# Column sums of k taken in column tiles directly behind the products they belong to, relu of the next k moved beside them, a sixth convolution bank, and GpSimd in a written order

## The chip, the cores and the metric

The kernel runs on one core of one Trainium2 chip. The metric is the device time of one launch in microseconds, the median of three runs. Everything is float32.

## The reference, cut to what matters

Two layers are applied to x of shape (8, 256, 64, 64). The first is an attention over keys and values that come from a strided 4x4 convolution; it is not touched here. The second is a linear attention with a multi-scale branch:

```python
qkv = einsum('oc,bchw->bohw', w_qkv, x)                     # 3 * 256 channels
dw  = depthwise 5x5 convolution of qkv, padding 2
agg = einsum('goi,bgihw->bgohw', w_pw, dw grouped by 8)     # 96 groups of 8
ms  = concatenate([qkv, agg], axis=1)
# per head of 8 channels: q, k, v of ms over the 4096 positions n
q, k = relu(q), relu(k);  v = [v, 1]                        # a column of ones
kv  = einsum('bhnd,bhne->bhde', k, v)                       # 8 x 9
out = einsum('bhnd,bhde->bhne', q, kv)
out = out[..., :-1] / (out[..., -1:] + 1e-15)
p   = einsum('oc,bchw->bohw', w_proj, att), scaled and shifted; result x + p
```

The ninth column of kv is the sum of relu(k) over all positions, since v is padded with ones. These column sums of k, once for the k of qkv ("raw") and once for that of the branch ("agg"), are what the change moves.

## The kernel before

The kernel has three passes. The first does layer one and stores q, k and v of the second layer in forms that the second can load. The second pass computes the convolved q and k and the sums kv. The third divides and projects.

The second pass works on 64 units, `(t, k, b)`: two halves of the channels, four groups of 32 channels in each, eight images. The function `second_pass` is a loop over `u`, in which unit `u` is convolved (k of the branch), unit `p = u - 1` has its sums taken, and pairs of units have their q convolved in "products" (`m`, one pair in two iterations). Thus an even iteration has four products and an odd one has five. One iteration on TensorE is:

- `convolve(u, 2)` (L1372), then `products(u, 0)` (L1403)
- `convolve(u, 0)`, then `products(u, 1)`
- `summed_raw(u)` (L1441): 32 matmuls of relu(k) against v in 32-wide column tiles, into the bank `raw`
- `summed(p)` (L1458): 32 matmuls with 288 columns in column tiles, into the bank `sums`
- `ended_raw(u)` (L1482): the column sum of raw k, one full-array matmul with `ones` as the weights' partner, into a column of `raw`
- `convolve(u, 1)`
- `ended(p)` (L1494): the column sum of the branch's k, one full-array matmul into the bank `few`
- `products(u, 2)`

Convolutions and products write to five banks tagged `cv`, in turn. With one bank each for `raw`, `sums` and `few` that is all eight.

GpSimd does, for each unit, three additions that fold k to one 128x128 block before its column sum (`reduced`: `red_raw` and `red_agg`, L1352 to L1354), the copy `c` of `paired(u, 2)` (L1299), and half of each `y` of `down` (L1325): `y_1` from the loaded grid `d`, `y_0` and `y_2` from differences `c0` that VectorE made in `across` (L1309). Once for each set of weights it also makes a quarter of the product weights `w` (`widened_q`, L603); VectorE makes another quarter and ScalarE, in 16 small activations (L613), the rest. These 18 steps are "chores" handed out by `do(n)` at fixed places of the iteration; `wide` marks the iterations with a set of product weights, and the other chores are `widened_k` (L592).

ScalarE applies relu to k in place (`positive`, L1359), copies and relus the convolution results (L1381, L1389, L1409). VectorE adds up what comes out of the banks (L1388, L1421, L1428, L1431), and turns `sums` into kv with `taps` (L1468 to L1475). SP issues every load and store: `d` for the k convolution (L1259), `kq` (L1273) and eight `vq` loads (L1285), two halves of `d` for the products (L1267), and the stores of kv (L1490, L1500) and q (L1508).

The order on each engine is made by a scheduler from its own estimate of when operands are ready. `tc.keep_in_program_order(i)` is an exception: it sets `i` behind the one instruction that was written just before it for the same engine. A pin on an instruction whose predecessor is itself free therefore pins it to little.

Of the kernel before, what the change touches and what calls it, by code (L numbers as in the profile page):

```python
# [29 lines left out]
ALU = mybir.AluOpType  # L30
# [568 lines left out]
def widened_q(tc, w, wd, ws):  # L599
    nc = tc.nc  # L600
    n = w.shape[1]
    for g in (2, 3):
        (nc.vector if g == 2 else nc.gpsimd).tensor_tensor(  # L603
            w[:, :, g].rearrange("p n (o f) -> p n o f", o=D1),
            wd[:, g].unsqueeze(2).to_broadcast([P, n, D1, R * R]),
            ws[:, g].unsqueeze(1).unsqueeze(3).to_broadcast([P, n, D1, R * R]),
            ALU.mult,
        )
        yield
    for g in (0, 1):  # L610
        for o in range(D1):
            tc.keep_in_program_order(
                nc.scalar.activation(  # L613
                    w[:, :, g, o * R * R : (o + 1) * R * R], wd[:, g], AF.Copy, scale=ws[:, g, o : o + 1]
                )
            )
            yield
# [595 lines left out]
def second_pass(ctx: ExitStack, tc: tile.TileContext, a, planes, kd, vd, kept, first_w, kvd, kvg, qd, ahead):  # L1213
    nc = tc.nc
    B = a.x.shape[0]
    def pool(name, bufs=1):
# [8 lines left out]
    )  # L1225
    psums = {
        tag: ctx.enter_context(tc.tile_pool(name=f"psum_{tag}", bufs=1, space=bass.MemoryType.PSUM))
        for tag in ("cv", "raw", "sums", "few")
    }

    def bank(tag, name, bufs=1, n=512):
        return psums[tag].tile([P, n], F32, tag=tag, name=name, bufs=bufs)
# [59 lines left out]
    def paired(u, i):  # L1292
        d = grids[u]
        c = cells[u, i] = pairs.tile([P, 4, (NB + 1) * NB // 2], F32, tag=f"c1_{i}", name=f"c1_{u}_{i}")
        v = c.rearrange("p g (y x) -> p g y x", x=NB // 2)
        d0, d1, d2 = (d[:, :, :, i : i + NB - 1 : 2] for i in range(3))
        if i == 2:

            nc.gpsimd.tensor_copy(v, d1)  # L1299
        else:  # L1300
            nc.vector.tensor_sub(v, d2 if i else d0, d1)

# [13 lines left out]
    def down(m, j):  # L1316


        c = column(m, j).rearrange("p g b y x -> p (g b) y x")
        y = quads.tile([P, 2, 4, P], F32, tag="y", name=f"y_{m}_{j}", bufs=2)  # L1320
        setattr(quad[m], f"y{j}", y)
        v = y.rearrange("p i g (b y x) -> p i (g b) y x", b=2, y=NB // 2)
        c0, c1, c2 = (c[:, :, i : i + NB - 1 : 2] for i in range(3))
        nc.vector.tensor_sub(v[:, 0], c0, c1)
        nc.gpsimd.tensor_tensor(v[:, 1], c2, c1, ALU.subtract)  # L1325

    load_cells(0)
    load_tokens(0)
# [15 lines left out]
    ones = const.tile([P, 1], F32, tag="ones", name="ones")  # L1344
    nc.vector.memset(ones, 1.0)

    kts, reds, raws, mraws, state, maggs = {}, {}, {}, {}, {}, {}


    def reduced(u, what, t):  # L1350
        r = mid.tile([P, 4, P], F32, tag=f"red_{what}", name=f"red_{what}_{u}", bufs=1)
        nc.gpsimd.tensor_tensor(r, t[0], t[1], ALU.add)  # L1352
        nc.gpsimd.tensor_tensor(r[:, :2], r[:, :2], r[:, 2:], ALU.add)
        nc.gpsimd.tensor_tensor(r[:, 0], r[:, 0], r[:, 1], ALU.add)  # L1354
        reds[u, what] = r[:, 0]

    def positive(u):
        kq = kqs[u]
        tc.keep_in_program_order(nc.scalar.activation(kq, kq, AF.Relu))  # L1359
        reduced(u, "raw", (kq[:, 0], kq[:, 1]))  # L1360

    def convolve(u, i):
        t, k, b = units[u]
        c, w = cells[u, i], wt[t, k]
        ps = bank("cv", f"cv1_{u}_{i}", 5)
        for g in range(4):
            for da in range(2):
                n = 2 * da + i if i < 2 else 4 + da  # L1370
                cols = slice(da * (NB // 2), da * (NB // 2) + P)
                nc.tensor.matmul(  # L1372
                    ps[:, g * P : (g + 1) * P],
                    c[:, g, cols],
                    w[:, g, n * P : (n + 1) * P],
                    start=(da == 0),
                    stop=(da == 1),
                )
        if i == 2:
            both = between.tile([P, QB], F32, tag="both", name=f"both1_{u}")  # L1380
            nc.scalar.copy(both, ps)  # L1381
            r = (second if u % 2 else sides).tile([P, 2, 4, P], F32, tag="r1", name=f"r1_{u}", bufs=1)
            state[u] = (r, both)
            kts[u] = r
        else:
            r, both = state[u]
            s = sides.tile([P, QB], F32, tag="s", name=f"s1_{u}_{i}")
            nc.vector.tensor_add(s, ps, both)  # L1388
            nc.scalar.activation(r[:, i].rearrange("p h n -> p (h n)"), s, AF.Relu)  # L1389


    def product(m, i, j):
        t, k, b = units[2 * m]
        now, w = quad[m], wq[t, k, (i, j)]
        ps = bank("cv", f"cv0_{m}_{i}{j}", 5)
        for g in range(4):
            out = ps[:, g * P : (g + 1) * P]
            if i == 1:
                x = column(m, j)[:, g, :, 1:NB:2]
                out = out.rearrange("p (b y x) -> p b y x", b=2, y=NB // 2)  # L1400
            else:
                x = getattr(now, f"y{j}")[:, i // 2, g]
            nc.tensor.matmul(out, w[:, g], x, start=True, stop=True)  # L1403

        def piece(name):
            return quads.tile([P, QB], F32, tag=name, name=f"{name}_{m}")

        def finished(v, y, x):
            nc.scalar.activation(  # L1409
                now.r.rearrange("p h b (y i x k) -> p i k (h b) y x", y=NB // 2, i=2, k=2)[:, y, x],  # L1410
                v.rearrange("p (n y x) -> p n y x", y=NB // 2, x=NB // 2),
                AF.Relu,
            )

        if (i, j) == (1, 1):
            now.both = between.tile([P, QB], F32, tag="both", name=f"both0_{m}")
            nc.scalar.copy(now.both, ps)
        elif j == 1:
            v = piece(f"side{i}")
            setattr(now, f"side{i}", v)  # L1420
            nc.vector.tensor_add(v, ps, now.both)  # L1421
        elif i == 1:
            now.r = now.r if j else late.tile([P, 4, 2, NK], F32, tag="r0", name=f"r0_{m}")
            for y in (0, 2):
                side = getattr(now, f"side{y}")
                v = side if j else piece(f"part{y}")
                setattr(now, f"part{y}", v)
                nc.vector.tensor_add(v, ps, side)  # L1428
        else:
            v = getattr(now, f"part{i}")  # L1430
            nc.vector.tensor_add(v, v, ps)  # L1431
            finished(v, i // 2, j // 2)


    def summed_raw(u):
# [11 lines left out]
                )  # L1447
        raws[u] = ps


    def summed(u):
        kt, vq = kts.pop(u), vqs.pop(u)
# [2 lines left out]
        for i in range(8):  # L1455
            par, r, c = i // 4, i // 2 % 2, i % 2
            for h in range(4):
# [4 lines left out]
                    start=(i == 0),  # L1462
                    stop=(i == 7),
                )
        t, k, b = units[u]
        reduced(u, "agg", (kt[:, 0].rearrange("p h n e -> p n h e"), kt[:, 1].rearrange("p h n e -> p n h e")))
        p = small.tile([P, 36, D1], F32, tag="p", name=f"p_{u}", bufs=1)
        nc.vector.tensor_mul(p, ps[:, : 36 * D1].rearrange("p (n e) -> p n e", e=D1), taps[t][:, k])  # L1468
        s = small.tile([P, D1], F32, tag="kv", name=f"kv_{u}")
# [3 lines left out]
        nc.vector.tensor_mul(x, mix[:, 4 * t + k], s.unsqueeze(1).to_broadcast([P, D1, D1]))  # L1473
        m = small.tile([P, D1 + 1], F32, tag="m", name=f"m_{u}")
        nc.vector.tensor_reduce(m[:, :D1], x, AX.X, ALU.add)  # L1475
        maggs[u] = m

    def ended_raw(u):
        t, k, b = units[u]
        ps = raws.pop(u)  # L1480
        col = ps[:, 64:65]
        nc.tensor.matmul(col, reds.pop((u, "raw")), ones, start=True, stop=True)  # L1482
        m = small.tile([P, D0 + 1], F32, tag="mraw", name=f"mraw_{u}")
        nc.vector.tensor_copy(m[:, :D0], ps[:, :D0])
        nc.vector.tensor_copy(m[:, D0:], col)
        mraws[u] = m

    def stored_raw(u):
        t, k, b = units[u]
        tc.keep_in_program_order(nc.sync.dma_start(kvd[b, t][:, k], mraws.pop(u)))  # L1490

    def ended(u):
        col = bank("few", f"few_{u}")[:, :1]
        nc.tensor.matmul(col, reds.pop((u, "agg")), ones, start=True, stop=True)  # L1494
        nc.vector.tensor_copy(maggs[u][:, D1:], col)

    def stored_agg(u):
        t, k, b = units[u]
# [30 lines left out]
        j = t + 2 * what  # L1529
        parts[j, k] = factors(nc, kept if what else w_q, a, j, k, 6 if what else 9)  # L1530

    positive(0)
    load_factors(0, 0)
    for i in (2, 0, 1):
        paired(0, i)
    for u in range(n_all + 3):
        p, q = u - 1, u - 2
        now, was, conv = u < n_all, 0 <= p < n_all, 0 <= q < n_all
# [14 lines left out]
        if conv and u % 2 == 0:  # L1553
            across(q // 2, 0)
            down(q // 2, 1)
        if u < 2:
            chores.append(weights_q(0, u))
        if now:
# [16 lines left out]
        if u == n_all:  # L1575
            next(ahead)
        if u == n_all + 1:
            ahead.send(lambda name: bank("cv", name, 5))
        if conv and u % 2:
            down(q // 2, 2)  # L1580
        products(u, 0)
# [6 lines left out]
            down(q // 2, 0)  # L1588
            across(q // 2, 2)
        products(u, 1)  # L1590
        do(3 if wide else 2)
        if now:
            summed_raw(u)
        if was:
            summed(p)
        if now:
            ended_raw(u)
            do(6 if wide else 2)
            convolve(u, 1)
        if u + 1 < n_all:  # L1600
            paired(u + 1, 1)
# [3 lines left out]
            load_tokens(2)  # L1605
        if was and p == n_all // 2 - 1:
            load_taps(1)
        if was:
            ended(p)
        products(u, 2)  # L1610

        if u + 1 < n_all:
            positive(u + 1)
        do(9 if wide else 0)
    ahead.send(lambda name: bank("cv", name, 5))

# [472 lines left out]
```

## Time and profile before

| | |
|---|---|
| median of 3 runs | 3550.98 us (3549.43 to 3553.87) |
| profiled execution | 3553.7 us, span 3551.9 us |
| TensorE matmuls busy | 3473.5 us, 98% of the span |
| VectorE, ScalarE, GpSimd busy | 2286.0 (64%), 1478.6 (42%), 1854.5 (52%) |
| mean granted TensorE clock | 0.990 |
| DMA | 647.28 MB, mean 182 GB/s; about 260 GB/s in the second pass |
| second pass | first convolution at 1931.50 us, last sums near 2902 us |

In the lines of the profile, `PE` is TensorE's matmul, `PEld` its weight load, `DVE` VectorE, `ACT` ScalarE, `POOL` GpSimd and `SPq` SyncE's DMA queue. A line of the timeline has start, duration of the merged group, engine, source line, operation, output and inputs, shape and count, and in brackets the idle time ahead of it with what ended it. Matmul ends are modelled, so lengths on TensorE are best read from start to start. One float32 matmul shows as two records. A line of waits has the waiter, what it waited for, microseconds in total, times and the longest.

### The profile page before, as it was taken

What the parts mean: (1) busy time and instruction counts of PE and PEld (TensorE: products, weight loads), DVE (VectorE), ACT (ScalarE), POOL (GpSimd) and SP (SyncE); (2) the same over time, 40 slices, a digit from 0 to 9 for tenths busy, and PEclk for the clock granted to TensorE, in tenths of its full rate; (3) what the DMA queues carried; (4) which work ended last, traced back from release to release, by engine and by line L of the source; (5) the groups of instructions that cost most, each with busy time, mean ns of one, the idle gap of its engine ahead of it and who ended that gap; (6) DMA issues with size and microseconds to landing.
All of it is one profiled execution on the core that took longest, in us unless ns stands there. A gap on an engine that the chain in (4) does not pass through costs nothing.

```text
span 3551.9 us, 91328 instructions
## 1 busy us (share of the span) xinstructions
PE 3473.5 (98%) x38050; PEld 2110.9 (59%) x38050; DVE 2286.0 (64%) x3507; ACT 1478.6 (42%) x3385; POOL 1854.5 (52%) x1754
## 2 busy tenths in 40 slices
PE   7999999999999999999998999999999999999998
PEld 5554655555545555555445888888888873343333
DVE  1567576576675765756777777777777784444443
ACT  2445344353453543535553444444444322333332
POOL 2556466465564664655664566565656542222221
PEclk9999999999999999999999999999999998999999
DMA  5445446355354463553656999999999988788773
GB/s 174 111 104 163 116 114 173 99 159 148 100 161 117 115 172 99 159 148 103 161 126 157 266 262 259 263 258 260 262 263 256 261 233 229 215 242 235 227 225 95
DMA packets 577192, 647.28 MB, mean 182 GB/s; under 512 B 81664, under 2 KB 452864, under 8 KB 576768
## 3 DMA queue, kind: packets, MB, share of 16 engines
q1 hardware_dynamic: 576768, 641.34, 64.9%
q8 instruction: 301, 4.93, 0.6%
q14 instruction: 123, 1.01, 0.1%
HBM read 389.85 MB, written 249.23 MB: 180 GB/s over the span
## 4 chain that ended last, share of the span: by engine, by line
PE 86%; DMA 5%; DVE 3%; SPq 2%; ACT 2%; issue 1%; POOL 1%; DVEq 0%; ACTq 0%; POOLq 0%
PE qkv L994 16%; PE p L1806 12%; PE sc L847 8%; PE cv L1372 7%; PE av L879 7%; PE sr L750 6%; PE o L947 6%; PE q L829 6%; PE cv L1403 6%; PE sums L1458 6%; DMA vq<-v 2%; PE av L905 2%; PE rep L1790 2%; DMA d<-planes 1%; PE den L1771 1%; PE raw L1441 1%
## 5 line engine op out<-in xcount | busy, mean ns | idle before, releaser
L860 ACT ACTIVATE e<-sc 128x512 f32<-128x512 f32 x1024 | 528.6, 603 | 508.3 <-PE sc L847 508.3
L899 POOL TENSOR_TENSOR ef<-ef,e 128x512 f32<-128x512 f32 x512 | 688.3, 1354 | 91.1 <-ACT e L860 67.8
L892 POOL TENSOR_TENSOR ef<-e 128x512 f32<-128x512 f32 x256 | 329.6, 1307 | 544.2 <-ACT e L860 544.1
L1372 PE MATMUL cv<-w,c 128*128 128x128 f32 x3072 | 385.2, 278 | 6.7 <-DVE stage L1007 4.0
L1816 POOL TENSOR_TENSOR y<-z,xs 128x512 f32<-128x512 f32 x120 | 156.9, 1307 | 427.0 <-ACT z L1814 413.1
L1372 PEld LDWEIGHTS cv<-w,c 128*128 128x128 f32 x3072 | 362.6, 193 | 8.5 <-issue 4.1
L847 PE MATMUL sc<-q,kk 32*64 32x256 f32 x8192 | 298.5, 387 | 5.6 <-ACT e L860 5.2
L994 PE MATMUL qkv<-differences,combined 128*128 128x512 f32 x576 | 288.7, 592 | 0.6 <-POOL differences L964 0.6
L926 DVE STREAM_TRANSPOSE rden<-av 128x256 f32<-128x256 f32 x256 | 99.7, 428 | 283.8 <-ACT att L917 236.3
L1458 PE MATMUL sums<-vq,r 128*32 128x288 f32 x4096 | 266.1, 408 | 0.8 <-issue 0.8
L1389 ACT ACTIVATE r<-s 128x512 f32<-128x512 f32 x128 | 80.9, 632 | 422.3 <-DVE s L1388 419.9
L1814 ACT ACTIVATE z<-p,bn 128x512 f32<-128x512 f32 x128 | 99.5, 777 | 372.9 <-PE p L1806 372.9
L879 PE MATMUL av<-e,vv 64*32 64x256 f32 x8192 | 252.4, 379 | 0.1
L847 PEld LDWEIGHTS sc<-q,kk 32*64 32x64 f32 x8192 | 155.3, 131 | 163.0 <-issue 101.4
L1806 PE MATMUL p<-raw,wp 128*128 128x512 f32 x512 | 247.5, 605 | 2.2 <-ACT wp L1742 2.2
L750 PE MATMUL sr<-x,wsr 128*128 128x256 f32 x1024 | 237.2, 385 | 11.6 <-DMA wsr<-in_w_sr_dram 11.6
L829 PE MATMUL q<-x,wq 128*128 128x512 f32 x512 | 241.9, 594 | 0.0
L1806 PE MATMUL p<-agg,wp 128*128 128x512 f32 x512 | 240.4, 592 | 0.0
L750 PEld LDWEIGHTS sr<-x,wsr 128*128 128x128 f32 x1024 | 196.3, 193 | 67.5 <-issue 40.9
L947 PE MATMUL o<-att,wout 128*128 128x512 f32 x512 | 230.3, 592 | 0.0
L932 DVE TENSOR_TENSOR att<-att,rall 128x512 f32<-128x512 f32 x128 | 217.6, 1700 | 4.4
L1010 DVE TENSOR_TENSOR whole<-part,qkv 128x512 f32<-128x512 f32 x256 | 172.3, 683 | 66.1 <-ACT part L1060 49.4
(164 smaller groups left out, 6073.9 us busy)
## 6 DMA issues: line engine op xcount, KB each, us to landing
planes<-stage SPq DMA_DIRECT2D x128, 578.0 KB
d<-planes SPq DMA_DIRECT2D x128, 578.0 KB
vq<-v SPq DMA_DIRECT2D x256, 256.0 KB
raw<-planes SPq DMA_DIRECT2D x64, 578.0 KB
x<-in_xp_dram SPq DMA_DIRECT2D x64, 512.0 KB
wsr<-in_w_sr_dram SPq DMA_DIRECT2D x128, 256.0 KB
x<-x SPq DMA_DIRECT2D x128, 256.0 KB
k<-turned SPq DMA_DIRECT2D x256, 128.0 KB
```

The lines of the kernel that those rows point to most:

```text
L750: nc.tensor.matmul(ps[:, oc], w[:, ci, oc * P : (oc + 1) * P], strips(b, f // 2)[:, ci, f % 2 * NK : (f % 2 + 1) * NK], start=(f == ci == ...
L829: nc.tensor.matmul(ps, consts["wq"][:, ci, c * P : (c + 1) * P], strips(b, s)[:, ci], start=(ci == 0), stop=(ci == 1),)
L847: nc.tensor.matmul(scs[h][HALVES[half], QH[kq % 2]], kks[b][rows, c, kq * P // 2 : (kq + 1) * P // 2], qs[rows, QH[half]], start=True, sto ...
L860: nc.scalar.activation(e[:, h % 2].rearrange("p q n -> p (q n)"), scs[h], AF.Exp, scale=D0**-0.5)
L879: nc.tensor.matmul(sums["av"][half][cols, : QB // 2], vvs[b][rows, kq, c * P + h * D0 : c * P + (h + 1) * D0], es[h // 2][rows, h % 2, kq ...
L892: tc.keep_in_program_order(nc.gpsimd.tensor_tensor(f, e[:, :, 0], e[:, :, 1], ALU.add))
L899: tc.keep_in_program_order(nc.gpsimd.tensor_tensor(f, f, e[:, :, half], ALU.add))
L947: nc.tensor.matmul(ps, consts["wout"][:, c, oc * P : (oc + 1) * P], att[c], start=(c == 0), stop=(c == 1))
L994: nc.tensor.matmul(ps, w, x, start=True, stop=True)
L1372: nc.tensor.matmul(ps[:, g * P : (g + 1) * P], c[:, g, cols], w[:, g, n * P : (n + 1) * P], start=(da == 0), stop=(da == 1),)
L1458: nc.tensor.matmul(ps[h * D0 : (h + 1) * D0, : 36 * D1].rearrange("p (r n e) -> p r n e", r=3, e=D1), kt[:, par, h, 2 * r + c], vq[:, r : ...
L1806: nc.tensor.matmul(as_block(ps, i // 2), wp[:, i, oc * P : (oc + 1) * P], block(g, i // 2, i % 2, j), start=(i == 0), stop=(i == 3),)
```

## The change

Six things are done, all in `second_pass`.

- The two column sums become `counted`: four matmuls each, one per 32-column tile, with one column of output, written to a free column of the bank of the products they belong to (`raw`, column 32; `sums`, column 288). Both stand right behind `summed(p)`. The bank `few` is gone, and the kv tail reads the column from the `sums` bank; raw kv is copied in one piece of 33 columns.
- The bank that came free goes to the convolutions: six `cv` banks.
- `reduced_agg(p)` is written near the start of the iteration, where before the additions were written behind `summed(p)`.
- `positive(u + 1)` and `reduced_raw(u + 1)` move from the end of the iteration to just behind the column sums, ahead of `convolve(u, 1)`. For unit 0 they are written behind `load_factors` and `paired`.
- The chores of an iteration stand 3, 3, 13 (wide) or 2, 2, 4, all ahead of the sums, where they were 3, 3, 3, 6, 9 or 2, 2, 2, 2.
- Every GpSimd instruction of the pass is pinned with `keep_in_program_order`: `c`, `y`, the `red` additions and `w`.

```diff
@@ widened_q
-        (nc.vector if g == 2 else nc.gpsimd).tensor_tensor(
+        made = (nc.vector if g == 2 else nc.gpsimd).tensor_tensor(
...
+        if g == 3:
+            tc.keep_in_program_order(made)
@@ second_pass
-        for tag in ("cv", "raw", "sums", "few")
+        for tag in ("cv", "raw", "sums")
...
+    pinned = tc.keep_in_program_order
...
-            nc.gpsimd.tensor_copy(v, d1)
+            pinned(nc.gpsimd.tensor_copy(v, d1))
...
-        nc.gpsimd.tensor_tensor(v[:, 1], c2, c1, ALU.subtract)
+        pinned(nc.gpsimd.tensor_tensor(v[:, 1], c2, c1, ALU.subtract))
...
     def positive(u):
         kq = kqs[u]
         tc.keep_in_program_order(nc.scalar.activation(kq, kq, AF.Relu))
+
+    def reduced_raw(u):
+        kq = kqs[u]
         reduced(u, "raw", (kq[:, 0], kq[:, 1]))
...
-        ps = bank("cv", f"cv1_{u}_{i}", 5)
+        ps = bank("cv", f"cv1_{u}_{i}", 6)
...
+    def counted(ps, at, red):
+        for j in range(4):
+            cols = slice(j * D0, (j + 1) * D0)
+            nc.tensor.matmul(ps[cols, at : at + 1], red[:, cols], ones, start=True, stop=True)
+
+    def reduced_agg(u):
+        kt = kts[u].rearrange("p q h (n e) -> p q h n e", n=4)
+        reduced(u, "agg", (kt[:, 0].rearrange("p h n e -> p n h e"), kt[:, 1].rearrange("p h n e -> p n h e")))
...
+        sums[u] = ps
+
+    def ended(u):
         t, k, b = units[u]
-        reduced(u, "agg", (kt[:, 0].rearrange("p h n e -> p n h e"), kt[:, 1].rearrange("p h n e -> p n h e")))
+        ps = sums.pop(u)
...
+        nc.vector.tensor_copy(m[:, D1:], ps[:, 36 * D1 : 36 * D1 + 1])
         maggs[u] = m
...
     def ended_raw(u):
-        ps = raws.pop(u)
-        col = ps[:, 64:65]
-        nc.tensor.matmul(col, reds.pop((u, "raw")), ones, start=True, stop=True)
         m = small.tile([P, D0 + 1], F32, tag="mraw", name=f"mraw_{u}")
-        nc.vector.tensor_copy(m[:, :D0], ps[:, :D0])
-        nc.vector.tensor_copy(m[:, D0:], col)
+        nc.vector.tensor_copy(m, raws.pop(u)[:, : D0 + 1])
         mraws[u] = m
...
-    def ended(u):
-        col = bank("few", f"few_{u}")[:, :1]
-        nc.tensor.matmul(col, reds.pop((u, "agg")), ones, start=True, stop=True)
-        nc.vector.tensor_copy(maggs[u][:, D1:], col)
...
-    positive(0)
     load_factors(0, 0)
     for i in (2, 0, 1):
         paired(0, i)
+    positive(0)
+    reduced_raw(0)
@@ the loop over u
+        if was:
+            reduced_agg(p)
...
         products(u, 1)
-        do(3 if wide else 2)
+        do(13 if wide else 4)
         if now:
             summed_raw(u)
         if was:
             summed(p)
         if now:
+            counted(raws[u], D0, reds.pop((u, "raw")))
+        if was:
+            counted(sums[p], 36 * D1, reds.pop((p, "agg")))
+        if u + 1 < n_all:
+            positive(u + 1)
+            reduced_raw(u + 1)
+        if now:
             ended_raw(u)
-            do(6 if wide else 2)
+        if was:
+            ended(p)
+        if now:
             convolve(u, 1)
...
-        if was:
-            ended(p)
         products(u, 2)
-
-        if u + 1 < n_all:
-            positive(u + 1)
-        do(9 if wide else 0)
```

Built, the two kernels have the same order in the first pass. On SP the two halves of the products' `d` stand ahead of the `vq` loads in the odd iteration, where before one half stood behind them. On VectorE `c0` and `y_1` of the next pair come early in the odd iteration. TensorE's products at a change of weights are no longer interleaved with a convolution.

## The prediction

> **What bounds the kernel now.** I read the page's busy shares first, then the engines by stage, then TensorE's instructions in order of time, then the list of who waited for whom. The change touches the second pass alone (about 1931 to 2905 us), so the stage table counts, not the whole span.
>
> ```profile
> core 0: us, PE busy (x) PEld busy (x) DVE busy (x) ACT busy (x) POOL busy (x), PEclk, DMA share, GB/s
> ...
> 2320.00:2440.00 120.00, 118.27 (x1732) 104.44 (x1730) 91.29 (x153) 51.55 (x115) 73.88 (x71) 1.00 0.94 265
> 2440.00:2560.00 120.00, 116.10 (x1713) 102.02 (x1714) 92.11 (x159) 52.20 (x116) 69.87 (x70) 1.00 0.91 256
> ```
>
> TensorE is busy 97 to 99% at full clock; VectorE has 24% spare, GpSimd 39%, the DMA engines 6 to 9%. So the second pass lasts as long as its TensorE stream, plus the few holes in it. One odd unit of that stream:
>
> ```profile
> 2355.51 0.73 PE L1441 MATMUL raw<-vq,kq 128*32 128x32 f32 x62
> ...
> 2356.09 4.07 PE L1458 MATMUL sums<-vq,r 128*32 128x288 f32 x62
> 2360.09 0.38 PE L1482 MATMUL raw<-ones,red_raw 128*128 128x1 f32 x2
> 2360.34 2.03 PE L1372 MATMUL cv<-w,c 128*128 128x128 f32 x16
> 2362.20 0.28 PE L1494 MATMUL few<-ones,red_agg 128*128 128x1 f32 x2
> 2362.34 1.14 PE L1403 MATMUL cv<-c,w 128*128 128x128 f32 x8
> 2363.32 1.95 PE L1372 MATMUL cv<-w,c 128*128 128x128 f32 x16
> 2365.11 1.95 PE L1403 MATMUL cv<-y,w 128*128 128x128 f32 x16
> 2366.89 1.95 PE L1372 MATMUL cv<-w,c 128*128 128x128 f32 x16
> 2368.68 1.06 PE L1403 MATMUL cv<-c,w 128*128 128x128 f32 x8
> 2369.57 1.06 PE L1403 MATMUL cv<-y,w 128*128 128x128 f32 x8
> ```
>
> Read start to start. The next raw begins at 2370.56, so this period is 15.05 us; the even one before it (2341.19 to 2355.51) is 14.32. A pair takes 29.37 and there is no hole in it. A convolution costs 1.79 and a product 0.89 where nothing disturbs them. The holes:
>
> ```profile
> POOL y L1325 <- DMA d<-planes: 81.6, 26, 10.7
> ...
> PE cv L1403 <- ACT w L613: 13.1, 7, 2.3
> ...
> PE few L1494 <- POOL red_agg L1354: 4.1, 1, 4.1
> ...
> PE cv L1403 <- DVE y L1324: 3.2, 2, 2.1
> ...
> PE cv L1372 <- DVE s L1388: 2.2, 1, 2.2
> ```
>
> [...]The seven waits for w lie one at each change of the product weights, every eight units. GpSimd's wait for d is the largest, but TensorE waits for nothing that comes of it.
>
> **The change part by part.**
>
> *Column sums.* Removed per unit: the two full-array sums. From the rows above: the first takes 2360.09 to 2360.34, 0.25; the convolution behind it 1.86 where 1.78 is clean, 0.08 more; the second 0.14; the product behind it 0.98 where 0.89 is clean, 0.09 more. Together 0.56. Added: two groups of four column-tile matmuls, 16 trace records, directly behind sums, so still in column tiles. The nearest row is raw, also 128*32: 64 records from 2355.51 to 2356.06, 8.6 ns each, so 0.14. Then the array goes back to the full width: the first sum cost 0.11 more than the second and stood at just that place, so 0.11, and the 0.08 behind it stays. New 0.33, gain 0.23 a unit, 64 units: **-15 us**. A rule speaks against this: the Trainium skill, "TensorE: Matmul & The Clock Gate", section "Wait — 56ns, not 53.3ns?", says that successive matmuls never start less than about 25 ns apart, however narrow. By it 16 records cost 0.40, the new total is 0.59, and the gain is nil. But the raw row runs at 8.6 ns across four column tiles, so I take the row; the rule gives the other end, 0. On the good side, were the way back free, 0.14 alone would gain 0.42 a unit, -27.
>
> *Weights.* The chores for the product weights (ScalarE L613, 16 a set) now stand 3, 3, 13 before the sums instead of 3, 3, 3, 6, 9; the last nine steps came at the unit's very end, which is why TensorE waited. Twelve activations of about 0.25 us now end about 12 us into the unit, some 4 us before the next unit's first product. From the chain of waits, the pairs of units with a weight change last 31.03, 32.25, 31.03, 34.25, 31.02, 32.25 and 33.82 between starts of sums, together 20.1 above seven clean pairs: the 13.1 of waiting, product matmuls of two banks interleaved to no use, one slow-clock stretch, and at 2441.85 a bank wait of 2.2 behind the reload of taps. In the changed order these products are whole again and a sixth bank is there. Against it, in these units GpSimd now does red_agg, c, w (1.08) and only then y_2: I charge 0.4 for each of seven, and leave 2 for the taps. **-15 us** (bounds -6 and -20).
>
> *GpSimd in set order.* Before, y_2 ran 6 us ahead of red_agg. Now the odd unit's order is red_agg, c, y_2, red_raw. From a unit start at 2363.32: red_agg started 0.52 in and took 1.29, 0.73, 0.46 with gaps, to 3.15; c 0.72; y_2 1.27, to about 5.2. The product that reads it starts 6.25 in. So nothing, with 1.0 us of cover; if the cover goes, each 0.1 beyond it costs 3.2 us over 32 odd units. In even units y_0 has about 10 us of cover. red_agg and red_raw both end some 5 us or more before their sums on TensorE, which now stand behind sums.
>
> *Relu of the next k.* One activation of 1.04 us is moved ahead of the second r; its load is issued right after raw of the unit before, about 14 us earlier, and in the chain of waits loads of this stage take 5.7 (d) to 7.2 us (vq) to land. Cost 0. If it were late, the r behind it on ScalarE, then red_agg and y_2 would be.
>
> *Queues.* On SP both halves of d now go ahead of the eight vq loads; before, the second went after them. VectorE accordingly does c0 and y_1 early in the odd unit, where it may wait up to 1 to 3 us for d. Behind it queue the evacuations of cv banks, but with six banks the nearest one needed is about 5 us off: cost 0. One 0.15 us copy less on VectorE: 0.
>
> *First units.* Here the pins hurt. kq(1) on ScalarE now stands behind 16 weight activations, these behind the wd additions on VectorE, and these behind s of unit 1, whose convolution ends at about 1950. I get kq(1) at 1958.5, red_raw(1) at 1961, red_agg(0) behind it at about 1964, and only then the sums and the next convolution, which waits for c on GpSimd too. Working on from there, the convolution that began at 1972.46 begins at about 1977. **+4.5 us** (bounds 0 and +8). The old 4.1 wait on red_agg is in this.
>
> *Last units.* VectorE takes the kvp additions before its s of unit 61, while their load was issued only at 2861.66: **+1** (0 to +3). The third pass keeps its order but for one swap of loads at its start: 0.
>
> Sum: -15 - 15 + 4.5 + 1 = -24.5. The profiled execution took 3553.7 (span 3551.9 and 1.8 around it), so 3529.2; it lies 2.7 above the median of 3551.0, so **3526 us**.
>
> **The rivals.** *Half is eaten* (late d, GpSimd waits of a few tenths, a longer first stretch): DMA share of 0.93 would rise to about 0.96 in the shorter pass. For: GpSimd's y waits on d in 26 places already. Against: the queue stands idle for 3.5 us before each vq, which shows room. Gain 12: 3539. *The 25 ns floor holds*: -15 drops out, 3541. *Slower, by one mechanism*: y_2 in set order becomes the bound of odd units. The same GpSimd shapes do stretch: red_agg's first step appears at 1.85, c at 1.17, y at 1.80. The Trainium skill, "SBUF — State Buffer", section "Who interferes with whom", calls the port that VectorE and GpSimd share an exclusive lock for a whole instruction, so a stretch by a whole VectorE operation is possible. All slowest at once give y_2 at 7.1, a wait of 0.85 and +27 us, which just cancels the gain. Slower begins at y_2 1.8 us later than worked out; at 2.1 it would be 1.1 times 32, +35: 3561. *It does nothing*: sums cost as before and the weight waits turn into GpSimd waits: 3550.
>
> **How the numbers follow.** Main case 0.66, 3526, own range 3513 to 3535. Half eaten 0.15, floor 0.10, slower 0.05, nothing 0.04. A measurement of this kernel can tell about 0.2%, 7 us, from no change. Main, half and floor lie beyond that: 0.91 faster; same 0.05, slower 0.04 (a part of the slower case ends inside the 0.2%). The range runs from the good side of the column sums with no loss in the first units (-27 - 15 + 1, 3510, taken as 3511) to the floor case with a little more, 3543.
>
> **What would show it.** Right: no few rows; 16 records 32x1 behind sums taking 0.1 to 0.2 us; unit pairs near 28.9; no wait of TensorE for w; a hole of 8 to 14 us near 1950 to 1964 for kq(1) and red_agg(0). Wrong: pairs at 29.3 or more; TensorE waiting for GpSimd's y each odd unit; these column sums taking 0.4 us; sums waiting for red_agg in the steady part.

## The result, and the profile after

The change is a gain, but less than half of the one forecast. The changed kernel takes 3541.69 us, median of 12 runs (3535.76 to 3549.73), against 3552.14 (3548.05 to 3555.07) for the kernel before on the same chip: ratio 0.9971, interval 0.9962 to 0.9980, so -10.4 us where -25 was forecast. On a second chip it was 3539.88 against 3550.22, again 0.9971 (0.9961 to 0.9982). The profiled execution took 3537.7 us (span 3535.8), 16 less than that of before.

The stage table of the changed kernel, with the columns of the one before:

```profile
core 0: us, PE busy (x) PEld busy (x) DVE busy (x) ACT busy (x) POOL busy (x), PEclk, DMA share, GB/s
2320.00:2440.00 120.00, 117.66 (x1845) 105.47 (x1845) 92.26 (x152) 54.78 (x124) 75.80 (x74) 1.00 0.96 268
2440.00:2560.00 120.00, 118.24 (x1915) 107.36 (x1918) 89.31 (x151) 53.76 (x126) 72.40 (x72) 1.00 0.98 276
```

DMA share, the mean busy share of the DMA engines, went from 0.94 and 0.91 to 0.96 and 0.98: the same bytes in a shorter time. The odd unit that the prediction shows, now in the changed kernel:

```profile
2355.49 0.73 PE L1448 MATMUL raw<-vq,kq 128*32 128x32 f32 x62
...
2356.08 4.07 PE L1473 MATMUL sums<-vq,r 128*32 128x288 f32 x62
2359.93 0.22 PE L1460 MATMUL raw<-ones,red_raw 128*32 128x1 f32 x6
...
2360.02 0.22 PE L1460 MATMUL sums<-ones,red_agg 128*32 128x1 f32 x6
2360.17 2.05 PE L1379 MATMUL cv<-w,c 128*128 128x128 f32 x16
2362.06 1.06 PE L1410 MATMUL cv<-c,w 128*128 128x128 f32 x8
...
2370.19 0.73 PE L1448 MATMUL raw<-vq,kq 128*32 128x32 f32 x62
```

Raw to raw is 14.70 us here (15.05 before) and 13.97 in the even unit ahead of it (14.32), so a clean pair takes 28.67 where 29.37 stood. Both column sums together last from 2359.93 to 2360.17, and the convolution behind them 1.89. The list of waits:

```profile
POOL red_raw L1356 <- ACT kq L1363: 244.4, 30, 11.3
...
DVE c L1313 <- DMA d<-planes: 81.1, 26, 5.4
...
PE cv L1410 <- POOL y L1329: 10.2, 6, 2.2
...
PE raw L1448 <- ACT kq L1363: 6.5, 1, 6.5
...
PE cv L1410 <- DVE y L1328: 3.4, 1, 3.4
...
PE cv L1410 <- DMA d<-planes: 2.0, 1, 2.0
```

TensorE no longer waits for w. At six of the seven weight changes it waits for GpSimd's y instead, 1.7 us each on average. As much waiting for d as GpSimd had before, 81 us, is now VectorE's.

The second pass can be measured from raw of unit 0 to raw of unit 63. Without any hole it would last 32 x 15.05 + 31 x 14.32 = 925.5 us before, and 32 x 14.70 + 31 x 13.97 = 903.5 in the changed kernel. What the profiled executions take above that, by place (first units: up to the fourth raw; weight changes: the two or three units at each; last units: from raw 59 on):

| us | clean | first units | weight changes | other | last units | raw 0 to raw 63 |
|---|---|---|---|---|---|---|
| before | 925.5 | 0.4 | 20.1 | 0.1 | 4.2 | 950.4 |
| changed | 903.5 | 6.2 | 16.4 | 0.3 | 8.9 | 935.3 |
| difference | -22.0 | +5.8 | -3.7 | +0.2 | +4.7 | -15.1 |

With -1.4 after raw 63 and +0.4 ahead of raw 0 this is the 16 us. The medians differ by 10.4; of the 5.6 us between, 4.0 lie between the changed kernel's profiled execution and its own median, and 1.6 on the side of before. The time of single runs goes with their granted clock (0.988 in the fastest of the twelve, 3535.76 us, and 0.985 in the slowest, 3549.73). Raw 0, ahead of which nothing was changed, starts at 1937.94 in this execution and at 1934.52 in another one of the same kernel, so lengths within the pass tell more than single spans.

A part of what is above clean is TensorE at a granted clock of 0.50. These are all such stretches between raw 0 and raw 63, in the columns of the stage table, two of the kernel before and then three of the changed one:

```profile
1953.30:1960.10 6.80, 4.76 (x25) 2.61 (x26) 6.77 (x11) 6.02 (x25) 5.43 (x6) 0.50 1.08 340
2806.70:2810.10 3.40, 3.40 (x36) 3.18 (x38) 2.18 (x4) 2.23 (x8) 2.04 (x4) 0.50 1.02 290
```

```profile
1954.00:1967.60 13.60, 6.41 (x109) 5.30 (x113) 6.42 (x11) 8.18 (x27) 10.13 (x11) 0.50 1.05 285
2090.50:2093.90 3.40, 3.40 (x83) 1.90 (x72) 1.65 (x2) 2.66 (x8) 3.24 (x5) 0.50 1.04 295
2821.00:2827.80 6.80, 3.37 (x23) 3.23 (x23) 6.80 (x8) 2.24 (x4) 6.64 (x5) 0.50 1.01 253
```

An estimate of their cost, half of TensorE's busy time in them, is 4.1 us before and 6.6 us in the changed kernel. So about 2.5 of the 7.0 us by which the changed kernel stands further above its clean time (31.8 us against 24.8) are the clock. (In stretches this short the DMA share can come out a little above 1.)

So the main question is why the weight changes, which were to give 15, gave 3.7.

### The profile page after: what moved, and what is told of

Read it like the earlier page. It is cut to its first block, busy times and chain, and to the rows that moved or that the text cites. A ratio compares the mean times of both kernels' runs of the same rounds, so it can differ in the third digit from the quotient of the medians.

```text
span 3535.8 us, 92804 instructions
## 1 busy us (share of the span) xinstructions
PE 3454.2 (98%) x38818; PEld 2111.5 (60%) x38818; DVE 2247.0 (64%) x3443; ACT 1472.4 (42%) x3385; POOL 1843.0 (52%) x1754
## 4 chain that ended last, share of the span: by engine, by line
PE 91%; DMA 3%; ACT 1%; POOL 1%; SPq 1%; DVE 1%; issue 1%; POOLq 0%; DVEq 0%; ACTq 0%
PE qkv L996 17%; PE p L1822 12%; PE cv L1379 9%; PE sc L849 8%; PE av L881 7%; PE cv L1410 6%; PE sums L1473 6%; PE sr L752 6%; PE o L949 6%; PE q L831 6%; PE av L907 2%; PE den L1787 1%; PE rep L1806 1%; PE raw L1448 1%; DMA vq<-v 1%
## 5 line engine op out<-in xcount | busy, mean ns | idle before, releaser
L1356 POOL TENSOR_TENSOR red_raw<-kq 128x512 f32<-128x512 f32 x64 | 83.4, 1304 | 309.5 <-ACT kq L1363 244.4
```

## The experiments

All times stand against the kernel before on the same chip (median 3550.83, 3552.25, 3550.22 and 3549.49 in the four groups).

**Column sums alone** (on the kernel before)

```diff
-        col = ps[:, 64:65]
-        nc.tensor.matmul(col, reds.pop((u, "raw")), ones, start=True, stop=True)
...
+            counted(raws[u], D0, reds.pop((u, "raw")))
...
+        counted(ps, 36 * D1, reds.pop((u, "agg")))
```

> The kernel before with the column sums alone changed: two groups of four column-tile matmuls behind sums, into the banks of raw and sums. Everything else, the chores, the five banks and the free order on GpSimd, stays. Theory (from the changed kernel's clean units, 13.97 and 14.70 us): each clean pair of units takes 28.67 us instead of 29.37, so 0.35 a unit and -22 us in all, 3530. Prediction on record: 0.23 a unit, pairs of 28.91, -15. The rule of 25 ns between starts: pairs of 29.37, no gain. The seven waits for w at the weight changes stay about as they were, 13 us together, in all three cases.

With these lines the additions of red_agg go to the start of the iteration and the kv tail to just behind the sums, as in the changed kernel; the convolutions keep five banks. 3546.67 us, ratio 0.9991 (0.9981 to 1.0001): no gain that can be told, although the clean pairs do take 28.67, so a sixth bank is not needed for that. Its weight changes cost 19.4 us, as was expected, but its first units 3.7, its last 9.7, and 4.8 went in small waits elsewhere (0.4, 4.2 and 0.1 before). Neither the theory nor the prediction had that. The profiled execution from which this is read, 3539.39 us, was the fastest of 22.

**Relu ahead of the activations** (on the changed kernel)

```diff
+        early = wide and 1 < u and u + 1 < n_all
+        if early:
+            positive(u + 1)
         do(13 if wide else 4)
```

> The changed kernel, with the relu of the next k placed ahead of the thirteen chores in the units that make product weights (from unit 2 on), so on ScalarE twelve weight activations (2.95 us) stand behind it instead of in front. GpSimd's set order is left as it is. Theory: in these units red_raw waits for that relu and y_1 stands behind red_raw in the set order, which is why TensorE waits 10.2 us in six places; with the relu 2.95 us earlier these waits go to nearly nothing, the six or seven extra pieces of about 2 us with them: -12 to -15 us against the changed kernel, about 3527 to 3530. Rival (the charge on record: y_2 or y_1 is late because w stands ahead of it on GpSimd): the waits stay, at most -3 us.

3534.60 us, 0.9953 (0.9940 to 0.9967), about 6 us less than the changed kernel. The weight changes fell from 16.4 to 4.4 as the theory said, with w still ahead of y on GpSimd, so w is not what made y late. But 8.5 us came up in units that had been clean: TensorE waited there for y or s, and VectorE's wait for d grew from 81.1 to 111.3. So the relu's place is not the whole cause.

**Unit 1 ahead of the first chores** (on the changed kernel)

```diff
-    positive(0)
-    reduced_raw(0)
+    for u in range(2):
+        positive(u)
+        reduced_raw(u)
```

> The changed kernel, with relu and red_raw of unit 1 placed with those of unit 0, ahead of the first chores. Theory: the 6.46 us in which TensorE waits for kq(1) and the 1.66 for red_raw(1) go; red_agg(0) is still behind w of the first set on GpSimd and leaves a wait of up to 3 us before the first column sums: -5 us (-3 to -8) against the changed kernel. Rival: the convolution behind waits for c on GpSimd and s on VectorE anyway, which the chores hold back too, then -1 or less.

3552.20 us, 1.0008 (0.9995 to 1.0021): some 12 us slower than the changed kernel. TensorE's waits for kq(1) and red_raw(1) went. In their place it waits 4.89 us (where the changed kernel waits 4.05 for VectorE) and 2.22 us for c on GpSimd, which now stands behind red_raw(1), and 6.42 for red_agg(0); the unit behind the first ones takes 4.2 us more than clean. The rival was right on what bounds this stretch, and neither saw the loss.

**Chores alone** (on the kernel before)

```diff
-        do(3 if wide else 2)
+        do(13 if wide else 4)
         if now:
             summed_raw(u)
...
-            do(6 if wide else 2)
...
-        do(9 if wide else 0)
```

> The kernel before with the chores alone moved (3, 3, 13 before the sums in wide units, 2, 2, 4 in the others); column sums, banks, relu and the free order on GpSimd stay. Theory: with GpSimd in free order y_1 of the weight-change units runs ahead of the late red_raw, so nothing takes the place of the waits for w, and most of the 20 us of the seven weight changes goes: -13 to -19 us against the kernel before. Rival: twelve activations in one piece ahead of r hold back the second r, red_agg and the sums as much as they gain: -5 or less, with TensorE waiting for red_agg, y or s in these units.

3536.77 us, 0.9960 (0.9948 to 0.9971). The weight changes cost 2.5 us instead of 20.1. So at the weight changes the move of the chores is worth what the prediction took from it and more, when nothing else is changed; 5.7 us of it went in the first units (2.8 where 0.4 stood) and the last (7.5 where 4.2 stood). Twelve activations ahead of the relu do no harm here, so they alone are not what the changed kernel loses by.

**Third pass's loads later** (on the changed kernel)

```diff
-    load_raw(0)
-    load_raw(1)
     yield
...
     yield
+    load_raw(0)
+    load_raw(1)
+    yield
```

> The changed kernel, with the four loads of the third pass's first two raw parts (2.4 MB) issued at unit 62, behind the last loads of the second pass, instead of at unit 59. Theory: they stand ahead of kq, vq and d of units 60 and 61 in the queue, so that d is late and TensorE waits 1.97 us for d and 3.43 for VectorE's y; raw to raw takes 22.9 us there where 13.97 is clean. Without them: -5 to -8 us against the changed kernel, about 3535. Rival: the eight vq loads themselves (13.1 us of queue at that place) make d late; then the wait stays within 2 us of what it is.

3540.86 us, 0.9971 (0.9961 to 0.9981), the same as the changed kernel. Unit 60 is clean, the last units cost 0.9 instead of 8.9, but what follows raw 63 takes 667.9 instead of 662.6, with 3.26 us of waiting for d in the very last products. So the wait was moved, not removed.

**Each column sum twice** (on the changed kernel)

```diff
-        for j in range(4):
+        for j in (0, 1, 2, 3, 0, 1, 2, 3):
```

> The changed kernel with each column-tile column sum issued twice, so 16 more records of TensorE in every unit. At the 8.6 ns a record that raw shows: 0.14 a unit, clean pairs of 28.95 us instead of 28.67, +9 us. At 25 ns from start to start: 0.40 a unit, pairs of 29.47, +26 us.

Clean units of 14.12 and 14.84, pairs of 28.95: 0.28 a pair for 32 records, 8.8 ns each. Median 3550.27, 0.9993 (0.9982 to 1.0004), 8 us more than the changed kernel where 9 was expected. The rule of 25 ns that the prediction cites does not hold across four column tiles.

**v loaded once** (on the changed kernel)

```diff
+        if u > 2:
+            vqs[u] = lasting[u % 3]
+            return
         vq = (first, odd, second)[u % 3].tile(
```

> The changed kernel with the loads of v left out after unit 2 (the three tiles of the first units are used again), so its values are not the reference's; it measures what the DMA queue costs. Eight of about twelve loads a unit and most of the bytes go; DMA share 0.95 should fall below 0.5. Theory: late d is what VectorE waits for (81 us in 26 places), and what TensorE waits for near the end; with the queue free these waits go, the 9 us at unit 60 with them, the 2 us at each weight change stay: -8 to -12 us against the changed kernel, and the runs lie closer together. Rival: d is late for another reason, no change beyond 2 us.

This kernel leaves out most loads of v, so its sums are not those of the reference. 3504.77 us, 0.9869 (0.9853 to 0.9885), 37 us less than the changed kernel where 8 to 12 were expected. A row of its stage table:

```profile
2320.00:2440.00 120.00, 120.00 (x1874) 108.36 (x1873) 94.52 (x157) 54.59 (x122) 78.69 (x74) 1.00 0.55 165
```

In this stretch DMA share is 0.55 and TensorE has no hole. The weight changes cost 0.4 us: they are clean with the relu still behind the twelve activations and y behind red_raw. "The 2 us at each weight change stay" was wrong, and that is the most useful miss of the set. VectorE's wait for d falls from 81.1 to 3.4 us, so the load to look at is d.

**First units as before, and both other edits** (on the changed kernel)

```diff
+        do(6 if u < 2 else 0)
...
+        if u < 2:
+            positive(u + 1)
+            reduced_raw(u + 1)
+            do(9)
+        SET_ORDER[0] = u > 0
```

> The changed kernel with three edits: relu of the next k ahead of the thirteen chores; the first two units with the chores, the relu's place and the free GpSimd order of the kernel before; the third pass's raw loads at unit 62. Theory: -9 (as relu_first's profiled execution shows), -4 to -5 (the stretch from the first raw to the fourth 45 us instead of 49.6), -5 to -8: together about -20 against the changed kernel, near 3522. If d is late whatever is moved, the second pass is bound by its loads, and the sum stays at -12 or less.

3535.36 us, 0.9955 (0.9942 to 0.9968): no better than relu_first alone. The first units still cost 4.3 us, the unit after them 4.2 more than clean (18.17), and what follows raw 63 takes 670.8 us instead of 662.6.

What reads d first? The order of VectorE in the traces tells. In the kernel before, c_0 (L1309) and y_1 stand behind the additions that empty the banks ("evacuations") `part` and `side`:

```profile
2185.59 1.44 DVE L1431 TENSOR_TENSOR part<-part,cv 128x512 f32<-128x512 f32 x2
...
2191.07 0.67 DVE L1431 TENSOR_TENSOR side<-side,cv 128x512 f32<-128x512 f32 x1
2192.43 1.29 DVE L1309 TENSOR_TENSOR c<-d 128x1088 f32<-128x1088 f32 x1 [0.69 <-DMA d<-planes]
```

In the changed kernel c_0 (L1313) stands between the two pairs of `part`. Nothing in the diff says so; the scheduler chose it. It stands there in cols_alone too, but not in chores_alone.

**c_0 back in its place** (on the changed kernel; `made` is c_0 in `across`, then VectorE's half of y_1 in `down`)

```diff
+        if j == 0:
+            pinned(made)
...
+            if j == 1:
+                pinned(made)
...
         if conv and u % 2 == 0:
-            across(q // 2, 0)
-            down(q // 2, 1)
+            down(q // 2, 1, (1,))
...
+        if u % 2 and u // 2 < n_all // 2:
+            across(u // 2, 0)
+            down(u // 2, 1, (0,))
```

> The changed kernel with one thing undone: VectorE's c_0 and its half of y_1, which read the newly loaded d, stand behind the evacuation side again, as in the kernel before, not between the two pairs of part ahead of it. GpSimd's set order, the relu's place and the chores are untouched. Theory: the 81 us in which VectorE waits for d (26 odd units, 3.1 each) hold back part, with it r on ScalarE, the twelve weight activations behind that, the relu, red_raw and y_1; with c_0 back the 2 us at each weight change go although y_1 still stands behind red_raw and the relu behind the activations: -10 to -15 us against the changed kernel, 3527 to 3532. Rival: the relu behind the activations is enough by itself, the 10 us of waits for y_1 stay, 0 to -3.

3527.32 us, 0.9935 (0.9920 to 0.9950), 12.6 less than the changed kernel on the same chip (0.9971, 0.9961 to 0.9982). Weight changes cost 1.1 us, other units 1.7; first and last units stay at 5.7 and 8.4. Here is one weight change in the changed kernel, rows of four engines' timelines, from raw at 2192.53 on:

```profile
2191.70 1.32 DVE L1313 TENSOR_TENSOR c<-d 128x1088 f32<-128x1088 f32 x1 [3.85 <-DMA d<-planes]
2192.95 1.27 DVE L1438 TENSOR_TENSOR part<-part,cv 128x512 f32<-128x512 f32 x2
...
2193.66 1.29 ACT L1416 ACTIVATE r<-part 128x512 f32<-128x512 f32 x2 [5.49 <-DVE part L1438]
...
2197.90 0.71 ACT L1416 ACTIVATE r<-side 128x512 f32<-128x512 f32 x1 [1.73 <-DVE side L1438]
2198.49 2.96 ACT L615 ACTIVATE w<-wd,ws 128x64 f32<-128x64 f32 x12
2201.35 1.04 ACT L1363 ACTIVATE kq<-kq 128x1024 f32<-128x1024 f32 x1
...
2202.47 1.31 POOL L1356 TENSOR_TENSOR red_raw<-kq 128x512 f32<-128x512 f32 x1 [10.59 <-ACT kq L1363]
...
2205.88 1.53 POOL L1329 TENSOR_TENSOR y<-d 128x512 f32<-128x512 f32 x1
...
2207.46 1.16 PE L1410 MATMUL cv<-y,w 128*128 128x128 f32 x8 [1.64 <-POOL y L1329]
```

And the same unit in c0_back, where its raw starts at 2183.91:

```profile
2184.98 0.67 DVE L1448 TENSOR_TENSOR side<-side,cv 128x512 f32<-128x512 f32 x1
2185.57 1.28 DVE L1313 TENSOR_TENSOR c<-d 128x1088 f32<-128x1088 f32 x1
...
2186.28 2.96 ACT L615 ACTIVATE w<-wd,ws 128x64 f32<-128x64 f32 x12
2189.14 1.04 ACT L1373 ACTIVATE kq<-kq 128x1024 f32<-128x1024 f32 x1
...
2190.26 1.28 POOL L1366 TENSOR_TENSOR red_raw<-kq 128x512 f32<-128x512 f32 x1 [6.98 <-ACT kq L1373]
...
2193.74 1.99 POOL L1339 TENSOR_TENSOR y<-d 128x512 f32<-128x512 f32 x1
...
2196.90 1.06 PE L1420 MATMUL cv<-y,w 128*128 128x128 f32 x8
```

Read the bracket in the first row of the changed kernel: VectorE stands 3.85 us for d, and behind it in its queue are part and side. ScalarE's r waits for those, the twelve activations stand behind r, the relu (`kq<-kq`) behind them, red_raw behind the relu, y behind red_raw. The relu starts 8.82 us after raw and y 13.35, at 2205.88, when TensorE has already come to the product that reads it (2207.46 less 1.64 is 2205.82). In c0_back the relu starts at 5.23 and y at 9.83, and the product at 12.99 finds it ready. VectorE's waits for d in the list of c0_back, where the changed kernel had 81.1 us:

```profile
DVE c L1313 <- DMA d<-planes: 13.2, 6, 5.2
```

**y_1 ahead of red_raw too** (on c0_back)

```diff
-            down(q // 2, 1, (1,))
...
-            down(u // 2, 1, (0,))
+            down(u // 2, 1)
```

> As c0_back, and GpSimd's half of y_1 is put ahead of red_raw of the next unit as well (the order that the kernel before ran in). Theory: if the late d alone is the cause, nothing more than c0_back gives, within 2 us; if the set order of GpSimd costs something by itself, 2 to 5 us more.

3524.10 us, 0.9926 (0.9911 to 0.9942); 921.4 us from raw 0 to raw 63 against 920.4 in c0_back. GpSimd's set order by itself costs nothing that can be told.

**And the relu first** (on c0_back_y1_early)

```diff
+        if early:
+            positive(u + 1)
         do(13 if wide else 4)
```

> As c0_back_y1_early, and the relu of the next k ahead of the thirteen chores in wide units. Theory: the relu's place no longer matters once VectorE does not wait for d: within 2 us of c0_back_y1_early, 3525 to 3530. If the activations were the cause, 5 us or more less.

3524.80 us, 0.9928 (0.9911 to 0.9944). The relu's place is worth about 6 us while VectorE waits for d, and nothing that can be told once it doesn't (3524.10 without it).

**The change again**

> The changed kernel as it is, on the same chip as the three others, to compare them directly and to have a second profiled execution: about 3541, with the waits for y_1 at the weight changes (10 us) and the 7 to 9 us at unit 60 again.

3539.88 us, as expected: 937.7 us from raw 0 to raw 63, 14.6 of it lost at the weight changes, 8.4 in the last units, and 5.5 in other units, where the first profiled execution lost 0.3. TensorE waits for y_1 in nine places here, three of them away from a weight change, so the split of the table changes by some us from one execution to the next.

**Column sums alone, c_0 back** (on cols_alone)

```diff
+        if j == 0:
+            tc.keep_in_program_order(made)
...
-            down(q // 2, 1)
+            down(q // 2, 1, (1,))
...
+            across(u // 2, 0)
+            down(u // 2, 1, (0,))
```

> The kernel before with the column sums alone changed, as in cols_alone, and VectorE's c_0 and its half of y_1 held behind the evacuation side, where the kernel before has them (cols_alone has c_0 ahead of part). Theory: cols_alone lost 70 us of VectorE's time to waiting for d in 23 units, and TensorE a part of that; with c_0 back the clean pairs of 28.67 us hold and the waits for w stay: -14 to -20 us against the kernel before, with 5 to 8 lost near unit 60. Rival: the column tiles disturb by themselves, then about -4 again.

3528.37 us, 0.9940 (0.9924 to 0.9956), 18 us less than cols_alone, with the last units costing 10.9. Better than expected: the weight changes cost 2.9 us without any chore moved. So VectorE's backlog behind d was most of what held back the weights in cols_alone as well: there, the last three activations of a set stand behind the relu and r, r behind VectorE's s and side. It is not the whole account of these waits: the kernel before has c_0 in this same place and loses 20.1 at the weight changes. What the column sums' edit adds to that was not taken apart.

**c_0 back, loads later**

> As c0_back_y1_early, with the third pass's first raw loads at unit 62 instead of 59. In the profiled execution of c0_back the unit up to raw 60 takes 22.3 us where 13.97 is clean. Theory: the queue has the same bytes to move before the end of the pass, so the wait moves to the last units, as in loads_later: raw 60 after 14 us, 5 to 8 us lost later, total within 3 us of c0_back_y1_early's 3524. If only the order of the loads were at fault: -6, 3518.

The edits are those of c0_back_y1_early and loads_later. 3526.77 us, 0.9936 (0.9920 to 0.9953), no better than c0_back_y1_early. Raw 60 comes after 13.98 us and the last units cost 1.3, but the rest after raw 63 takes 668.8 instead of 665.7 us, with 4.63 of waiting for d in it.

## Why the prediction was wrong

*Column sums, -15.* The mechanism was right and the size too small: -22.0. The term that failed is the switch from column tiles to the full array, which the sum charged to the new order, 0.11, and did not take off the old one. Before, sums lasted 4.00 us up to the first column sum; now 3.85. So the 4.00 held that switch, and what went is 0.71 a unit and not 0.56. What came was sized well: the two groups plus the way to the convolution take 0.24 and the convolution 0.11 more than clean, 0.35 where 0.33 was charged. The whole gain is 0.35 a unit, not 0.23. The row was right against the rule of 25 ns: sums_twice shows 8.8.

*Queues, cost 0: the step that failed.* The prediction saw that "VectorE accordingly does c0 and y_1 early in the odd unit, where it may wait up to 1 to 3 us for d". That happened: 81.1 us in 26 places, 3.1 each. What it asked was whether a cv bank would come free in time, and with six banks that was no matter. It did not follow the other reader of what VectorE makes: ScalarE's r, and all that stands behind r on ScalarE and then on GpSimd. c0_back takes the order of c_0 and VectorE's half of y_1 back and regains 12.6 us: that, and not 0, was the cost.

*Weights, -15.* It was -3.7. The gain itself is real (chores_alone: 20.1 to 2.5), but the charge of "0.4 for each of seven", for y_2 behind w on GpSimd, was put on the wrong instruction and too small. What became late is y_1, behind red_raw and the relu, by 0.55 to 2.22 us at six changes, and after the first of them came a stretch of slow sums.

*Relu of the next k, 0.* The price was right for a relu in the right place. Its load was no matter; the prediction looked at the load ahead of it and not at the queue ahead of it, which in these units holds the twelve activations. By itself that is harmless (c0_back has the relu in this place and loses 1.1 us at the weight changes); with a late d it is the link.

*GpSimd in set order, 0.* Right: y_2 in the odd units never became a wait, and the slower rival did not occur. Steps of GpSimd do stretch (red_raw's second one took 1.19 us at 2203.86 in the changed kernel, red_agg's 0.74 at 2209.21), but no run here shows whether the shared port does it.

*First units, +4.5.* Right in size: +5.8; the convolution forecast for about 1977 started there. This is luck in part. The work that was to wait for kq(1), red_raw(1) and red_agg(0) began at 1956.92, 1959.66 and 1962.21, not at 1958.5, 1961 and 1964; with 13.6 us at a clock of 0.50 from 1954.0 on, twice as long as before and not in the sum, it still came to 1977.51. The cure that suggests itself is none (head_first, combined).

*Last units, +1.* It was +4.7, for another reason: at unit 60 d is late behind the third pass's first loads, and VectorE and the product wait for it. The kernel before lost 4.4 us at the weight change two units earlier, which may have given the queue that time: chores_alone, which is clean at that change, lost 7.0 us at unit 60. No run tests this alone.

The rival "half is eaten" came nearest, 3539, and named late d, though as waits of GpSimd. It was put at 0.15 because "the queue stands idle for 3.5 us before each vq". What stands idle there is the queue that issues the loads; DMA share in the same stage was 0.94. Nor does idle time on average show that d lands in time for an instruction that was moved ahead.

With c_0 back the total, -22.9 us, is near the forecast, but by other terms: in the profiled execution, which took 8.4 us less than the median, -22.0 for the column sums, -19.0 at the weight changes, and +9.5 in the first and last units.

Left open: what sets the granted clock of a run (on the second chip the mean over the runs was 0.9893 before and 0.9871 for the changed kernel), and why the scheduler placed c_0 early in this kernel and in cols_alone but not in chores_alone.

## What to carry to other kernels

- When a change shifts the order on an engine, follow every reader of what now stands behind a possible wait, through the second and third engine, not only the buffers. Here one read of d that was moved ahead of two evacuations cost 12.6 us, most of what the weights' move was to bring.
- Two gains that end the same wait don't add: chores_alone gained 14 us, cols_alone_c0_back 21, and both together with c_0 in place (c0_back) 23, because each of the first two alone already cleared most of the weight changes (2.5 and 2.9 us left of 20.1).
- Where a scheduler decides, compare the order on each engine after every edit, and pin what matters. c0_back and c0_back_y1_early beat both kernels, at 3527 and 3524 us.

## What was not expected of the hardware

With the loads of v left out, DMA share 0.55 in place of 0.96, the changed kernel lost 8.1 us to holes between raw 0 and raw 63 where it had lost 31.8, although its TensorE work was the same. A queue at 0.95 of its time is not what the pass is bound by (long runs of units are clean at 28.67 a pair), but with it d lands late enough that the place of its first reader decides: c0_back moves that reader back at a full queue and clears the weight changes too.

A hole in TensorE can cost more than its length. After the one of 2.22 us at the first weight change, sums of the next unit show 5.54 us where 4.07 is usual, and the clock granted for 3.4 us from 2090.5 on is 0.50. After the five other waits for y it was 1.00, though one of these was as long; in change_again two of nine were followed by such a stretch. What decides it, these runs do not show.
